# Layer 3 of a four-layer cross-attention and feed-forward network: the experts' work placed in steps between the attention slots of the next chunk, gelu from tanh, four engines in the source's order

## The chip, the cores and the metric

The kernel runs on one core of a Trainium2 chip. The metric is the device time of one execution in microseconds (us); lower is better. A core has TensorE (matrix products into PSUM), VectorE, ScalarE (activations), GpSimd[...] and DMA queues, here all issued by SyncE. Each engine works through its own queue of instructions and waits for the others through semaphores. In the profile the engines are called PE, PEld (TensorE's weight loads), DVE (VectorE), ACT (ScalarE), POOL (GpSimd) and SP (SyncE).

## What is computed

A stream `x` of 2048 tokens by 256 features passes four layers. Each adds a cross-attention over 1601 context rows and then a feed-forward part, both on the layer-normalized `x`:

```python
x = x + L0_xattn(layernorm(x), ctx);  x = x + L0_ffn(layernorm(x))
x = x + L1_xattn(layernorm(x), ctx, mask);  x = x + L1_ffn(layernorm(x))
x = x + L2_xattn(layernorm(x), ctx);  x = x + L2_ffn(layernorm(x))
x = x + L3_xattn(layernorm(x), ctx, ctx, mask);  x = x + L3_ffn(layernorm(x))

# L3_xattn: 16 heads of 16
weights = softmax(where(mask == 0, -inf, Q @ K.T / 4))
return (weights @ V) @ Wo.T + bo

# L3_ffn: 8 experts, each with its own 256 consecutive tokens
h = gelu(tokens @ w1 + b1)          # 256 -> 1024, jax.nn.gelu, the tanh form
y = h @ w2 + b2                     # 1024 -> 256
```

The change touches layer 3 alone (the last two lines of the network). The mask lets each query see only context rows from number 1201 on, so the kernel has a path that works with the 400 rows of that tail.

## The kernel before

All matrix products are in float32, except the one for the softmax maxima, which is in bfloat16. The tokens are worked on in four chunks of 512 (`CH`), a chunk has four tiles of 128 (`TPC`), and `self.x` holds the 16 tiles in SBUF.

**Attention of layer 3, `attention3_tail` (L1415).** The 16 heads form four groups `g` of four heads, each head in its own 32 partitions. A *unit* `u` is a pair (chunk, group): 16 units. The 400 keys are cut into four pieces `kt` of 100. The main loop (L1635) has 64 *slots*, n = 4u + kt. In a slot stand, in this order of the source:

- `scores(u, kt)` (L1560): four matmuls of 512 columns, one for each head, into two PSUM tiles `psc` (two banks each), and two exponentials on ScalarE (L1571) to the tiles `p3`.
- `maxima(n+6, 0)` and `maxima(n+6, 1)` (L1538): for a unit that is one and a half units ahead, two bfloat16 matmuls (L1546) into a `psc` tile, and VectorE's reduction to the maxima (L1550). `values` of the slot before stands between the two.
- `values` (L1574): four matmuls of the exponentials with the values into the bank `pa`. After a unit's last one, ScalarE copies `pa` to `o3` (L1587), and `normalize` is put on the list `tasks`.
- one of: `project(u+2)` in slots with kt = 0 (L1524: a query projection into the bank `pm`, and two ScalarE copies with bias); `shift(u+1)` with kt = 2 (L1554: transposes of the maxima into `pm`, one VectorE addition); or, in the other slots, a task: `normalize` (L1590: a matmul into `pm`, and a ScalarE copy to `ri3`), or one or two steps of the list `later`, which holds `out_project`.
- a piece of `reciprocal` (L1600: 128 columns of `ri3` on VectorE; after the fourth piece a product on GpSimd, L1606, and after a chunk's last unit four `out_project` on the list `later`).
- `out_project(c, i)` (L1610): four matmuls into `pm`, an addition of the bias on GpSimd (L1618), one of PSUM and `x` on VectorE (L1619).
- once per chunk `normed` (L1621): `norm` (L125) for the next chunk: statistics on VectorE (L132, L133), the inverse root on GpSimd (L135, L136), scaling on VectorE (L142), eight transposes into `pm` and two copies on ScalarE (L161, L165).

[...]L1517 gives three `psc` tiles of two banks, one `pm`, one `pa`. L1518 keeps TensorE in the source's order; the order of the other engines' instructions is chosen by a scheduler.

**Experts, `ffn3` (L1669).** It comes after the attention. For each expert `e` the weights come by DMA (three sets of buffers); for every second expert `norm` runs. Eight *up* products (L1702, two matmuls of 256 columns each) are followed by a gelu activation with bias on ScalarE (L1706, function Gelu_apprx_tanh) to `h3`; then for each of two token tiles eight *down* matmuls (L1713) gather in `pa`; GpSimd adds `x` and the bias `b2` to `y` (L1718), VectorE adds `pa` (L1719), and a DMA writes `y` out (L1720). There are two `y` buffers.

Of the kernel before, what the change touches and what calls it, by code (L numbers as in the profile page):

```python
# [14 lines left out]

P = 128
D = 256
NTOK = 2048
NCTX = 1601
NT = NTOK // P  # L20
CH = 512
# [8 lines left out]
TK = 4  # L30
# [9 lines left out]
def drain(gen):  # L40
    if gen is not None:
        for _ in gen:
            pass


def step(gen, n):
    if gen is None:
        return
    for _ in range(n):
        if next(gen, True):  # L50
            return


class Net:
# [70 lines left out]
    def norm(self, c, row_scale=None, rms=False, split=None):  # L125


        nc = self.nc
        st = self.small.tile([P, TPC, 6], F32, name="st")
        mv = self.small.tile([P, TPC, 2], F32, name="mv")  # L130
        for i in range(TPC):
            nc.vector.bn_stats(st[:, i, :], self.x[c * TPC + i])  # L132
            nc.vector.bn_aggr(mv[:, i, :], st[:, i, :])  # L133
        rstd = self.small.tile([P, TPC], F32, name="rstd")
        nc.gpsimd.tensor_scalar_add(rstd, mv[:, :, 1], LN_EPS)  # L135
        nc.gpsimd.tensor_tensor(rstd, rstd, self.mhalf, ALU.pow)  # L136
        if row_scale is not None:
            nc.gpsimd.tensor_tensor(rstd, rstd, row_scale, ALU.mult)
        xns = []
        for i in range(TPC):  # L140
            xn = self.xnp.tile([P, D], F32, name="xn", bufs=4)
            nc.vector.tensor_scalar(  # L142
                xn, self.x[c * TPC + i], mv[:, i, 0:1], rstd[:, i : i + 1], ALU.subtract, ALU.mult
            )
            xns.append(xn)
        if rms:
            ss = self.small.tile([P, TPC], F32, name="ss")
            for i in range(TPC):
                sq = self.xnp.tile([P, D], BF16, name="sq", bufs=1)
                nc.scalar.activation(sq, xns[i], AF.Square, accum_out=ss[:, i : i + 1])  # L150
            ri = self.rms_inverse(ss, D)
            for i in range(TPC):
                nc.vector.tensor_scalar(xns[i], xns[i], ri[:, i : i + 1], None, ALU.mult)
        if split is None:
            xnT = self.xnp.tile([P, 2, CH], F32, name="xnT")
        else:
            xnT = [split.tile([P, 2, CH], F32R, name=f"xn{n}") for n in ("hi", "lo")]
        for kc in range(2):
            ps = self.pm()
            for i in range(TPC):  # L160
                nc.tensor.transpose(  # L161
                    ps[:, i * P : (i + 1) * P], xns[i][:, kc * P : (kc + 1) * P], self.ident
                )
            if split is None:
                nc.scalar.copy(xnT[:, kc, :], ps)  # L165
            else:
                nc.scalar.copy(xnT[0][:, kc, :], ps)
                nc.vector.tensor_tensor(xnT[1][:, kc, :], ps, xnT[0][:, kc, :].bitcast(F32), ALU.subtract)
        return xnT

    def rms_inverse(self, ss, n):

# [1239 lines left out]
                        nc.vector.tensor_tensor(x, ps[:, :D], x, ALU.add)  # L1412


    def attention3_tail(self, mask):  # L1415
        tc, nc, a = self.tc, self.nc, self.a
        H, DH, G = 16, 16, 4
        raw = {}
# [3 lines left out]
        with ExitStack() as s:  # L1422
            kv = s.enter_context(tc.tile_pool(name="kv3", bufs=1))
            qp = s.enter_context(tc.tile_pool(name="q3", bufs=3))
            pp = s.enter_context(tc.tile_pool(name="p3", bufs=6))
            op = s.enter_context(tc.tile_pool(name="o3", bufs=2))


# [42 lines left out]
            with ExitStack() as s0:  # L1471
# [4 lines left out]
                nc.gpsimd.memset(v.rearrange("p k (h e) -> p (k h) e", e=32)[:, :, DH : DH + 1], 1.0)  # L1476
                self.transpose_weight(wkT, raw["Wk"], pad=True)
                self.transpose_weight(wqT, raw["Wq"], pad=True)
                wvT = kv.tile([P, 2, D], F32, name="wvT")
                self.transpose_weight(wvT, raw["Wv"])  # L1480
                nc.vector.tensor_copy(
                    wop.rearrange("p o (h e) -> p (o h) e", e=32)[:, :, 0:DH],
# [31 lines left out]
                        bv[:TR].rearrange("p (h e) -> p h e", e=DH), ALU.add,  # L1514
                    )

            self.banks(s, s=3, m=1, a=1)  # L1517
            s.enter_context(tc.manual_schedule(engines={mybir.EngineType.PE}))  # L1518
            units = [(c, g) for c in range(NCH) for g in range(G)]
            U = len(units)  # L1520
            heads = [slice(32 * j, 32 * j + 32) for j in range(4)]
# [88 lines left out]
            def out_project(c, i):  # L1610
                x = self.x[c * TPC + i]
                ps = self.pm()
                for k in range(G):
                    nc.tensor.matmul(  # L1614
                        ps[:, :D], lhsT=attn[c][:, k, i * P : (i + 1) * P], rhs=woT[:, k, :],
                        start=k == 0, stop=k == G - 1,
                    )
                nc.gpsimd.tensor_tensor(x, x, bo, ALU.add)  # L1618
                nc.vector.tensor_tensor(x, ps[:, :D], x, ALU.add)  # L1619

            def normed(c):  # L1621
                xnT[c] = self.norm(c)


            tasks, later, pieces = [], [], []
            normed(0)
            for u in range(2):
                project(u)
            for n in range(6):
# [4 lines left out]
            last = None  # L1634
            for n in range(U * TK):  # L1635
                u, kt = divmod(n, TK)
                scores(u, kt)
                maxima(n + 6, 0)
                if last is not None:
                    values(*last)  # L1640
                last = (u, kt)
                maxima(n + 6, 1)
                if kt == 0 and u + 2 < U:
                    project(u + 2)
                elif kt == 2 and u + 1 < U:
                    shift(u + 1)
                elif tasks:
                    f, args = tasks.pop(0)
                    f(*args)
                elif later:  # L1650
                    f, args = later.pop(0)
                    f(*args)
                    if kt == 3 and later:
                        f, args = later.pop(0)
                        f(*args)
                if pieces:
                    reciprocal(*pieces.pop(0))
                if n % (G * TK) == TK and u // G + 1 < NCH:
                    normed(u // G + 1)
            values(*last)  # L1660
            for f, args in tasks:
                f(*args)
            for args in pieces:
                reciprocal(*args)
            for f, args in later:
                f(*args)


    def ffn3(self):  # L1669
# [53 lines left out]
@with_exitstack  # L1723
def network(ctx: ExitStack, tc: tile.TileContext, a, out):
    net = Net(ctx, tc, a, out)
    net.load_context()
    masks = ("mask_BxSxS2_ik0", "mask_1x1xSxS2_ik0")
    with tc.tile_pool(name="look", bufs=2) as pool:
        net.attention0(net.look_at_masks(pool, masks))
    net.experts0()  # L1730
    n_odd = net.verdict()
    with tc.If(n_odd == 0) as masked:
        net.attention1_tail("L1_xattn", masks[0])
        net.ffn1()
        net.attention1("L2_xattn", bias=True)
        net.ffn2()
        net.attention3_tail(masks[1])
        net.ffn3()
    with masked.Else():
        net.attention1("L1_xattn", mask=masks[0])  # L1740
        net.ffn1()
        net.attention1("L2_xattn", bias=True)
        net.ffn2()
        net.attention3()
        net.ffn3()
# [35 lines left out]
```

## Time and profile before

| what | us |
|---|---|
| median of 3 runs | 2220.4 (2210.71 to 2221.96) |
| the profiled execution | 2223.65 |
| its span, first to last instruction | 2221.9 |
| first exponential of layer 3's attention | at 1781.7 |
| last exponential of it ends | at 2087.8 |
| stretch with experts alone | 2107.0 to 2221.9 |

The profile's page gives the engines' share of the whole span:

```profile
PE 1968.0 (89%) x8841; PEld 967.7 (44%) x8841; DVE 1209.1 (54%) x2252; ACT 717.5 (32%) x968; POOL 632.3 (28%) x405
...
PEclk9799999999998699999997899999978889799999
```

The first line has busy us, share and number of instructions for each engine. The second cuts the span into 40 equal slices and shows in tenths which share of TensorE's full clock was granted; layer 3 fills about the last eight of them. The shares are means over stages with different limits, so that layer 3 has to be read from its own stretches.

### The profile page before, as it was taken

Reading aid. Unit: us, or ns where it says so; the run is one execution under the profiler, and the core shown is the slowest. Engines: PE = TensorE matmul, PEld = TensorE weight load, DVE = VectorE, ACT = ScalarE, POOL = GpSimd, SP = SyncE. Lnnn points to the kernel's source line nnn. Section 1 sums busy time; section 2 is a strip of 40 time slices with the busy share of each in tenths; the row PEclk is TensorE's granted clock in tenths of the full one; section 3 lists DMA queues with packets and bytes.
Section 4 is the critical chain, followed back from the end, with each engine's and each line's share of the span. In section 5 each row is a group of like instructions: output and inputs, shape, how many; then the busy total and the mean of one; then the engine's idle time right before and its main releaser. Section 6 shows DMA issues by size and latency. Waiting matters only on the chain.

```text
span 2221.9 us, 22832 instructions
## 1 busy us (share of the span) xinstructions
PE 1968.0 (89%) x8841; PEld 967.7 (44%) x8841; DVE 1209.1 (54%) x2252; ACT 717.5 (32%) x968; POOL 632.3 (28%) x405
## 2 busy tenths in 40 slices
PE   7789999999998677789897889999968788989899
PEld 3233333333334422234443674555557422333487
DVE  4565646555552599975645563222076557566500
ACT  4544434344443100000112442111143255455422
POOL 1168878777785000000000021000024401000100
PEclk9799999999998699999997899999978889799999
DMA  8820000000000000000201000000000000000351
GB/s 278 265 83 1 1 1 1 1 1 1 1 1 0 1 0 1 1 0 0 67 0 40 0 1 21 0 1 1 0 0 1 6 1 1 1 1 1 114 188 61
DMA packets 39698, 63.51 MB, mean 29 GB/s; under 512 B 5133, under 2 KB 32158, under 8 KB 39582
## 3 DMA queue, kind: packets, MB, share of 16 engines
q1 hardware_dynamic: 37776, 60.33, 8.4%
q10 hardware_dynamic: 1806, 1.64, 0.2%
q8 instruction: 71, 1.16, 0.2%
q14 instruction: 45, 0.37, 0.1%
HBM read 59.87 MB, written 2.10 MB: 28 GB/s over the span
## 4 chain that ended last, share of the span: by engine, by line
PE 66%; DVE 22%; ACT 4%; issue 3%; DMA 3%; POOL 2%; SPq 0%; DVEq 0%; ACTq 0%; POOLq 0%
PE pa L454 7%; PE psc L442 5%; PE psc L627 5%; PE psc L766 4%; PE pa L786 4%; DVE ge L576 4%; DVE mp L367 4%; PE psc L1564 3%; PE psc L1702 3%; DVE ge L578 2%; PE pa L1713 2%; DVE ri L404 2%; PE pa L1581 2%; DVE ri L1604 2%; PE pm L1614 2%
## 5 line engine op out<-in xcount | busy, mean ns | idle before, releaser
L463 POOL TENSOR_TENSOR sp<-sp,p 128x1024 f32<-128x1024 f32 (+1 forms) x176 | 418.9, 2380 | 59.6 <-ACT p L447 49.0
L367 DVE TENSOR_REDUCE mp<-pm 128x1 f32<-128x512 f32 x384 | 242.6, 679 | 161.4 <-PE pm L362 160.7
L447 ACT ACTIVATE p<-psc 128x1024 f32<-128x1024 f32 (+1 forms) x208 | 212.9, 1024 | 261.1 <-PE psc L442 167.0
L442 PE MATMUL psc<-qT,kT 64*128 64x512 f32 (+1 forms) x832 | 219.9, 591 | 0.0
L454 PE MATMUL pa<-p,v 128*64 128x512 f32 (+1 forms) x832 | 204.2, 613 | 0.0
L593 PE MATMUL psc<-ge,pick 128*8 128x512 bf16 x512 | 142.3, 378 | 37.9 <-DVE ge L576 18.6
L1571 ACT ACTIVATE p<-psc 100x1024 f32<-100x1024 f32 x128 | 125.5, 1023 | 110.1 <-PE psc L1564 104.5
L1550 DVE TENSOR_REDUCE ms<-psc 128x2 bf16<-128x800 f32 x128 | 124.1, 987 | 67.2 <-PE psc L1546 63.0
L362 PE MATMUL pm<-kb,qb 64*128 64x512 bf16 x384 | 100.2, 389 | 26.4 <-DVE mp L367 24.9
L1564 PE MATMUL psc<-q,kT 32*100 32x512 f32 x512 | 97.8, 689 | 14.8 <-DVE ms L1550 10.3
L627 PE MATMUL psc<-w_e,xe 128*128 128x512 f32 x256 | 110.4, 593 | 0.0
L454 PEld LDWEIGHTS pa<-p,v 128*64 128x64 f32 (+1 forms) x832 | 51.1, 137 | 131.6 <-issue 128.6
L135 POOL TENSOR_SCALAR rstd<-mv 128x4 f32<-128x4 f32 x32 | 10.5, 329 | 333.6 <-DVE mv L133 333.6
L829 POOL MEMSET v<- 128x4 f32 x1 | 0.1, 106 | 366.4 <-DVE n_odd L280 366.4
L766 PE MATMUL psc<-q,kT 128*128 128x512 f32 (+1 forms) x208 | 102.2, 610 | 0.0
L576 DVE TENSOR_SCALAR ge<-bc,g 128x128 bf16<-128x128 f32 (+15 forms) x128 | 99.8, 780 | 1.8 <-ACT bc L570 1.8
L142 DVE TENSOR_SCALAR xn<-x,mv,rstd 128x256 f32<-128x256 f32 x128 | 54.3, 482 | 75.0 <-PE pm L161 72.1
L442 PEld LDWEIGHTS psc<-qT,kT 64*128 64x128 f32 (+1 forms) x832 | 85.5, 185 | 19.5 <-issue 6.3
L786 PE MATMUL pa<-v,p 128*128 128x257 f32 (+1 forms) x416 | 93.9, 381 | 0.0
L593 PEld LDWEIGHTS <-pick 128*8 128x8 bf16 x512 | 39.4, 85 | 117.3 <-issue 91.3
L578 DVE TENSOR_SCALAR ge<-bc,g 128x1920 bf16<-128x1920 f32 (+14 forms) x120 | 89.4, 746 | 0.6 <-ACT bc L570 0.6
L440 PE MATMUL psc<-sh,negz 64*128 64x512 bf16 (+1 forms) x416 | 87.1, 383 | 2.6 <-ACT sh L389 2.5
(343 smaller groups left out, 3250.5 us busy)
## 6 DMA issues: line engine op xcount, KB each, us to landing
w<-in_L_ffn_w_dram SPq DMA_DIRECT2D x16, 1024.0 KB, 6.2
head<-in_mask_BxSxS_ik_dram SPq DMA_DIRECT2D x16, 600.5 KB, 4.7
head<-in_mask_1x1xSxS_ik_dram SPq DMA_DIRECT2D x16, 600.5 KB, 4.8
tail<-in_mask_BxSxS_ik_dram SPq DMA_DIRECT2D x16, 200.0 KB, 4.5
tail<-in_mask_1x1xSxS_ik_dram SPq DMA_DIRECT2D x16, 200.0 KB, 3.7
x<-in_x_dram SPq DMA_DIRECT2D x16, 128.0 KB, 3.7
w_e<-in_L_ffn_experts_dram SPq DMA_DIRECT2D x2, 1024.0 KB, 7.2
out_dram<-y SPq DMA_DIRECT2D x16, 128.0 KB, 2.7
```

The source lines that it names most:

```text
L367: nc.vector.tensor_reduce(mp[:, i, j, n : n + 1], pair[j][:, :wd], AX.X, ALU.max)
L442: nc.tensor.matmul(sc[:r, j, :], lhsT=kT[h, hp, kt * P : kt * P + r], rhs=q[h, :], start=False, stop=True,)
L447: nc.scalar.activation(p[:r], sc[:r], AF.Exp, scale=DH**-0.5)
L454: nc.tensor.matmul(acc[h, :], lhsT=v[:r, kt, hp * P + h.start : hp * P + h.stop], rhs=p[:r, j, :], start=kt == 0, stop=kt == NKT - 1,)
L463: nc.gpsimd.tensor_tensor(sums[:r], sums[:r], p[:r], ALU.add)
L576: nc.vector.tensor_scalar(ge[:, :hi], bc[:, :hi], own, None, ALU.is_lt)
L578: nc.vector.tensor_scalar(ge[:, hi:], bc[:, hi:], own, None, ALU.is_le)
L593: nc.tensor.matmul(rk[j // 2][0:E, j % 2, :], lhsT=pick[:, e, :], rhs=ge[:, j * CH : (j + 1) * CH], start=first, stop=last,)
L627: nc.tensor.matmul(sc[:, j, :], lhsT=xnT[t // TPC][:, kc, (t % TPC) * P : (t % TPC + 1) * P], rhs=ew[kc][:, half * 4 + 2 * j : half * 4 + ...
L766: nc.tensor.matmul(sc[:r, j, :], lhsT=kT[:, kc, ks], rhs=q[:, kc, :], start=kc == 0, stop=False)
L786: nc.tensor.matmul(acc[:, : D + 1], lhsT=p[:r, kt, i * P : (i + 1) * P], rhs=v[:r, kt, :], start=kt == 0, stop=kt == NKT - 1,)
L1564: nc.tensor.matmul(sc[j // 2][:TR, j % 2, :], lhsT=kT[h, g, kt * TR : (kt + 1) * TR], rhs=q[u][h, :], start=True, stop=True,)
```

## The change

- `norm` becomes a generator, `norm_steps`, of six steps; `norm` itself runs it through and gives the same instructions.
- `attention3_tail` and `ffn3` (in this path) become one function, `layer3_tail`. All four compute engines are kept in the source's order from the first norm of layer 3's attention on (`IN_ORDER`).
- When the last `out_project` of a chunk has been placed, the list `fbits` gets the chunk's expert work in 38 bits: `begin` and five `norm_step`, then for each of the chunk's two experts eight `up` (two matmuls and a ScalarE copy with bias) and eight `down` (two matmuls), a `down` being four places behind its `up`. Each slot of the loop takes two bits: `feed(1)` between the two maxima, and `feed(1)` at its end. What is left is placed after the loop.
- gelu is taken apart. ScalarE copies the up product with the bias to `h`; after each second `up` GpSimd works out z = h (1 + 0.044715 h²) in three instructions on 128x512; `gelu()`, in the slot after the second maximum, puts tanh(0.798 z) on ScalarE and (z + 1) h on VectorE. The factor 0.5 is in the last addition.
- PSUM: two `psc` tiles (for three), `pm`, `pa`, and one bank each for the up products (`psu`) and the down sums (`psy`).
- SBUF: five `p3` tiles (for six), two sets of expert weights (for three), one `y` (for two). The first two experts' weights are asked for before the loop, those of expert e + 2 when expert e ends.
- In a slot: a piece of `reciprocal` first, then `scores`, `values`, first maximum, fed bit, second maximum, `gelu()`, project, shift or task, one step of `later`, fed bit, one step of the next chunk's norm.

The diff, cut to its core:

```diff
+IN_ORDER = {mybir.EngineType.PE, mybir.EngineType.Activation, mybir.EngineType.DVE, mybir.EngineType.Pool}
...
-            self.banks(s, s=3, m=1, a=1)
-            s.enter_context(tc.manual_schedule(engines={mybir.EngineType.PE}))
+            self.banks(s, s=2, m=1, a=1)
+            psf = s.enter_context(tc.tile_pool(name="ps_f", bufs=1, space=bass.MemoryType.PSUM))
+            wp = s.enter_context(tc.tile_pool(name="f3w", bufs=2))
+            hp = s.enter_context(tc.tile_pool(name="f3h", bufs=2))
...
+            for e in range(2):
+                load_expert(e)
+            s.enter_context(tc.manual_schedule(engines=IN_ORDER))
...
+                if i == TPC - 1:
+                    fbits.extend(feed_forward(c))
...
+                def up(e, f, k):
...
+                    for kc in range(2):
+                        nc.tensor.matmul(
+                            ps, lhsT=w1[:, kc, (f + k) * P : (f + k + 1) * P],
+                            rhs=out[0][:, kc, (e % 2) * 256 : (e % 2 + 1) * 256],
+                            start=kc == 0, stop=kc == 1,
+                        )
+                    at = e * NF + f + k
+                    h = state["h"][:, f : f + 2, :]
+                    nc.scalar.activation(h[:, k, :], ps, AF.Identity, bias=b1[:, at : at + 1])
+                    if k == 1:
+                        z = hp.tile([P, 2, 256], F32, name="z3")
+                        nc.gpsimd.tensor_tensor(z, h, h, ALU.mult)
+                        nc.gpsimd.tensor_scalar(z, z, 0.044715, 1.0, ALU.mult, ALU.add)
+                        nc.gpsimd.tensor_tensor(z, z, h, ALU.mult)
+                        gelus.append((h, z))
...
+                def end(e):
+                    b2 = experts.pop(e)[2]
+                    for i in range(2):
+                        t = 2 * e + i
+                        y = hp.tile([P, D], F32, name="y", bufs=1)
+                        nc.gpsimd.tensor_tensor(y, self.x[t], b2, ALU.add)
+                        nc.vector.scalar_tensor_tensor(y, state["acc"][:, i, :], 0.5, y, ALU.mult, ALU.add)
+                        nc.sync.dma_start(self.out[0, t * P : (t + 1) * P, :], y)
+                    if e + 2 < E:
+                        load_expert(e + 2)
...
+                yield begin, ()
+                for _ in range(5):
+                    yield norm_step, ()
+                for e in (2 * c, 2 * c + 1):
+                    for f in range(0, NF + 4, 2):
+                        for k in range(2):
+                            if f < NF:
+                                yield up, (e, f, k)
+                        for k in range(2):
+                            if f >= 4:
+                                yield down, (e, f - 4, k)
...
+            def gelu():
+
+                if gelus:
+                    h, z = gelus.pop(0)
+                    nc.scalar.activation(z, z, AF.Tanh, scale=0.7978845608028654)
+                    nc.vector.scalar_tensor_tensor(h, z, 1.0, h, ALU.add, ALU.mult)
...
             for n in range(U * TK):
                 u, kt = divmod(n, TK)
+                if pieces:
+                    reciprocal(*pieces.pop(0))
                 scores(u, kt)
-                maxima(n + 6, 0)
                 if last is not None:
                     values(*last)
                 last = (u, kt)
+                maxima(n + 6, 0)
+                feed(1)
                 maxima(n + 6, 1)
+                gelu()
...
-                elif later:
+                if later:
                     f, args = later.pop(0)
                     f(*args)
...
+                feed(1)
+                if n % (G * TK) == 0 and u // G + 1 < NCH:
+                    norming = self.norm_steps(u // G + 1, xn)
+                step(norming, 1)
             values(*last)
+            feed(1)
+            gelu()
+            feed(1)
             for f, args in tasks:
                 f(*args)
-            for args in pieces:
-                reciprocal(*args)
-            for f, args in later:
+            while pieces:
+                reciprocal(*pieces.pop(0))
+                feed(2)
+                gelu()
+            while later:
+                f, args = later.pop(0)
                 f(*args)
+                feed(1)
+            while fbits:
+                ready = len(gelus)
+                feed(2)
+                for _ in range(ready):
+                    gelu()
...
-        net.attention3_tail(masks[1])
-        net.ffn3()
+        net.layer3_tail(masks[1])
```

## The prediction

> **What bounds the kernel now.** I read four views. First the table of stretches for the last stage: the span from the first exponential of layer 3 (1781.7) to the last one (2087.8), and what follows. Columns: busy us and (x instructions) of TensorE, its weight loads, VectorE, ScalarE, GpSimd; granted clock; DMA share; GB/s.
>
> ```profile
> 1781.70:1904.90 123.20, 110.46 (x598) 33.59 (x597) 76.72 (x92) 67.72 (x82) 12.28 (x13) 0.88 0.00 1
> 1904.90:2055.00 150.10, 137.45 (x731) 46.02 (x730) 95.90 (x122) 76.53 (x91) 12.66 (x12) 0.87 0.00 1
> 2055.00:2087.80 32.80, 29.46 (x182) 11.13 (x180) 16.24 (x26) 17.63 (x20) 3.80 (x4) 1.00 0.01 1
> 2087.80:2107.00 19.20, 14.78 (x73) 10.50 (x71) 11.14 (x25) 5.17 (x9) 2.88 (x5) 1.00 0.77 253
> 2107.00:2221.90 114.90, 110.60 (x512) 94.19 (x512) 8.17 (x20) 31.77 (x68) 11.22 (x15) 1.00 0.41 133
> ```
>
> The 64 attention slots take 306.1 us (4.8 each) with TensorE some 90% busy at a clock of 0.87, the last 134.1 us are a 19 us changeover and then experts that are TensorE alone at full clock (512 matmuls, 110.6 us, 13.8 per expert). GpSimd is nearly idle. So there is little empty TensorE time to put the experts into: about 30 us of gaps and what the clock loses.
>
> Second, the groups of instructions in the loop and in the expert stage, for durations (columns: busy, mean ns, idle before and its releaser):
>
> ```profile
> L1571 ACT ACTIVATE p<-psc 100x1024 f32<-100x1024 f32 x128 | 125.5, 1023 | 110.1 <-PE psc L1564 104.5 <-PE psc L1546 5.5
> L1550 DVE TENSOR_REDUCE ms<-psc 128x2 bf16<-128x800 f32 x116 | 113.2, 987 | 62.8 <-PE psc L1546 58.6 <-PE psc L1564 3.5
> L1606 POOL TENSOR_TENSOR attn<-o,ri 128x512 f32<-128x512 f32 x15 | 19.0, 1266 | 211.5 <-DVE ri L1604 205.1 <-ACT p L1571 6.4
> ...
> L1706 ACT ACTIVATE h<-psc,b 128x256 f32<-128x256 f32 x64 | 30.2, 474 | 66.0 <-PE psc L1702 66.0
> L1718 POOL TENSOR_TENSOR y<-x,b 128x256 f32<-128x256 f32 x16 | 11.6, 728 | 98.1 <-DMA out_dram<-y 64.4 <-issue 24.6 <-PE pm L161 9.0
> ```
>
> Third, the timeline of one slot: scores 1.12 us, a pair of exponentials starting 1.24 us after the scores, two reductions.
>
> ```profile
> 1862.64 1.12 PE L1564 MATMUL psc<-q,kT 32*100 32x512 f32 x8
> ...
> 1863.88 1.94 ACT L1571 ACTIVATE p<-psc 100x1024 f32<-100x1024 f32 x2 [0.54 <-PE psc L1564]
> ...
> 1866.74 1.83 DVE L1550 TENSOR_REDUCE ms<-psc 128x2 bf16<-128x800 f32 x2
> ```
>
> Fourth, stretches of 3.4 us: where four reciprocals in a row (3.4 us on VectorE) hold up the reductions, TensorE goes part idle and its clock is halved next.
>
> ```profile
> 1847.60:1851.00 3.40, 2.62 (x14) 0.57 (x16) 3.15 (x5) 1.02 (x1) 1.26 (x1) 0.82 0.00 0
> 1851.00:1854.40 3.40, 3.40 (x18) 0.87 (x19) 2.00 (x2) 1.02 (x1) 0.00 (x0) 0.50 0.00 0
> ```
>
> **What the Trainium skill says.** PSUM — Partial Sum Buffer, "Engine vs sequencer instructions": the queues of ScalarE, VectorE and GpSimd are strict FIFO; so an activation that waits holds all behind it. No row shows it directly, the new order makes it decisive. TensorE: Matmul & The Clock Gate, Part 1: an idle window halves the clock; the two lines above agree in kind (2.62 of 3.40 busy, then 0.50). ScalarE: Activation LUTs, "Table sets": exp and tanh share a set, gelu has its own; the trace has one 1.28 us table load before the first exponential and one before the first gelu (2105.24); the second goes.
>
> **The change part by part.** Times below are at full clock. Names: S scores 1.05, V values 1.0, M0 and M1 maxima 0.34 each, F1 and F2 the two fed bits of a slot (4 expert matmuls each, 6.91/8 = 0.86), X the slot's extra (project 1.98, shift 0.40, normalize 1.07), L an out-projection 2.0.
>
> *Slots with nothing fed (n = 0 to 24).* PSUM buffers for scores and maxima fall from three to two, so the second half of S waits for the reduction of M1: S 1.05, V 1.0, M0 0.39 to the start of its reduction, two reductions 1.83, hand-overs 0.1: 4.4 us. X, one reciprocal (0.91) and the norm steps fit beside. 25 x 4.4 = 110. The single bank for X, L and norm transposes makes L wait for X's copies: slots 21 to 24 cost 11 more, the transposes of the norm in 4, 5, 20 and 21 some 9 more. Sum 130, against 120.8 now (exponential of slot 0 at 1781.71, of slot 25 at 1902.54).
>
> *Where feeding falls.* A chunk's bits are begin, five norm steps, and per expert 8 up and 8 down: 38. The first is taken at the end of slot 24, so every bit with k=1 comes in the middle of a slot, and gelu() follows it in the same slot. Slots 25 to 63 hold 79 bits: chunks 0 and 1 (four experts) whole, and half of the experts' work is left for after the loop.
>
> *An up slot.* The tanh is put on ScalarE right behind the bias copy whose polynomial GpSimd has still to work out. From exponential to exponential: exponential 1.02, M0 0.40, up 0.86, to ScalarE 0.1, bias copy 0.47 (the gelu row's shape), GpSimd: two products of 1.27 (attn row), one tensor_scalar, hand-overs 0.25; tanh 0.61, next bias copy and hand-overs 0.6. The tensor_scalar on 128x512 is in no row: between 0.52 and 1.27 us; I take 0.62, that of a one-input GpSimd cast of this shape (L672). The tanh likewise: between the 0.586 of a copy and 0.685 with a bias column; I take 0.61. Sum 7.3 us. Behind the waiting tanh stand X's copies, the next bias copy and both next exponentials; M0 and the next up wait for those. TensorE needs some 5.5 of the 7.3. X's copies add 1.4 in a project slot, 0.6 in a normalize slot. 16 up slots in the loop: 16 x 7.3 + 6 x 1.4 + 4 x 0.6 - 8 x 0.4 (no bias copy follows) = 124. In slots 36, 37, 38, 40 and 56 L or a norm transpose needs the bank whose copy stands behind the tanh: 1.6 to 5.6 each, 19 together. 143.
>
> *A down slot* has no tanh: S, exponential, M0, F1, M1, F2 give 4.9, plus X (project 1.8, normalize 0.85, shift 0.2). 16 slots: 78, X 5, L in 39, 53, 54: 8. The last one of an expert ends it with y in one buffer: the second addition waits for the first y's DMA (2.7 to land) on GpSimd, the VectorE instruction behind it waits too, and M1's reduction with it: 4.5 more in three slots (in the fourth no reduction is left), 13.5; without reductions 3 less. 102.
>
> *Norm slots* (25 to 27, 44 to 46): VectorE steps of 1.0 to 1.2 between the two reductions: 35. Slot 63: 3.5.
>
> Loop: 130 + 143 + 102 + 35 + 3.5 = 414 against 306: +108.
>
> *After the loop.* Four experts remain. The same immediate gelu() stands between the last reciprocals, and the out-projections' bank is freed by VectorE behind the waiting products: expert 4 ends 38 us after the last exponential. In the last while loop products are taken an iteration later, so GpSimd bounds: y wait 4.3, four polynomials of 3.3, tanh to product 1.5, last down 1.8: 20.8 per expert (13.8 now). Expert 5 ends at 59; chunk 3's norm, behind the second y, ends at 72; expert 6 at 91, expert 7 at 112; two y in turn 7.5: 120 against 134: -14. The weights' DMAs (SP, 2.1 MB an expert, 6.2 to land) hide under the expert before; without that cover some 4 each.
>
> *Clock.* An up slot leaves TensorE idle up to 2.8 us at a stretch. Between nothing (all at full clock) and +86 (32 pairs of up at half clock, M0 and up 1.2 more on the chain: 38; and 16 down slots 3 more: 48). I take half of the pairs: +19.
>
> Sum: +108 - 14 + 19 = +113 on the profiled execution's span 2221.9 (its own time 2223.65; the runs' median is 2220.4): 2335.
>
> **The rivals.**
> - *The one-bank and y waits are hidden, the clock holds:* what the traces show for it is that now such waits (DMA out_dram, 64.4 us) cost nothing; against it, they stand in strict order now. Takes away 19 + 13.5 + 12 (y after the loop) of +94: 2271.
> - *TensorE goes cold through both parts:* for it, 0.50 already after a window 77% busy; against, the down slots are dense. +94 + 86: 2402.
> - *Faster: TensorE stays the bound at full clock, the polynomial done before the tanh is reached.* TensorE's work in the loop: 67 + 64 + 39 (S, V, M) + 51 (X) + 24 (L) + 7 (norms) + 55 (half of the experts) = 307, about today's 306, since the split reciprocals end the halved clock; afterwards GpSimd's 4 x 14.7 and 23 for start and end: 82 for 134. 2172. For it: GpSimd is idle and 13% of the clock is lost today. Against: the order of the bits. It decides once an up pair costs 2.9 us less than above (94/32), a slot of 4.4.
>
> **How the numbers follow.** Forecast 0.52, milder 0.20, colder 0.15, faster 0.13 (of which and of the milder case 0.03 within 0.5%). A measurement of this kernel tells a change from none at about 0.5%. Slower 0.85. The range 2260 to 2410 takes in the milder and colder cases and the bounds of the clock; the faster one is left out.
>
> **What would show it.** Right: in the loop ScalarE waits for GpSimd before each tanh some 3.4 us; up slots near 7.3 us, down slots near 5; VectorE waits for GpSimd's y, and that for the DMA, about 4 us per expert; expert 4 begins only after the loop; one table load fewer. Wrong: tanh without wait, slots under 5.3, GpSimd's polynomial well under 3 us, or a loop near 306 us with the clock at 1.0.

## The result, and the profile after

The kernel after the change takes 2361.35 us (median of 4 runs, 2350.77 to 2372.57), the kernel before, beside it, 2221.18. The ratio is 1.064 (95% interval 1.057 to 1.070): slower by 6%, where 2335 was predicted and 2260 to 2410 given as the range. The profiled execution is the slowest of the four, 2372.57 us; its span is 2370.7.

First the table of stretches of the kernel after, cut where the prediction's sums cut it: slots 0 to 24, slots 25 to 63 (in which experts are fed), and what follows the last exponential. The columns are those of the prediction's first table. In the kernel before, the same stretches took 120.8, 185.3 and 134.1 us, at a clock of 0.87, 0.90 and 1.00.

```profile
1775.80:1923.80 148.00, 123.49 (x607) 38.14 (x610) 77.08 (x108) 66.02 (x81) 10.34 (x12) 0.85 0.00 1
1923.80:2220.90 297.10, 241.33 (x1180) 108.00 (x1172) 129.78 (x177) 120.94 (x165) 73.87 (x79) 0.89 0.10 30
2220.90:2370.70 149.80, 94.85 (x312) 64.71 (x310) 32.01 (x60) 28.12 (x55) 62.51 (x67) 0.79 0.14 45
```

The loop has grown from 306.1 to 445.1 us. The slots in which nothing is fed yet went from 120.8 to 148, with nothing more to compute than before. And what follows the loop, although half of the experts' work is gone from it, did not shrink: 149.8 for 134.1, with TensorE at 0.79 of its clock where the experts had 1.00 before.

The groups of instructions in the loop, those that wait (busy us, mean ns of one | idle us ahead of them and what ended it):

```profile
L1580 PE MATMUL psc<-kb,qb 32*128 32x400 bf16 x232 | 40.2, 366 | 32.7 <-ACT p L1605 28.2 <-DVE ms L1584 3.9
...
L1692 POOL TENSOR_TENSOR z<-z,h 128x512 f32<-128x512 f32 x16 | 20.3, 1269 | 1.3
...
L1690 POOL TENSOR_TENSOR z<-h 128x512 f32<-128x512 f32 x16 | 16.8, 1048 | 118.1 <-ACT h L1687 118.1
...
L1735 ACT ACTIVATE z<-z 128x512 f32<-128x512 f32 x16 | 10.1, 630 | 51.5 <-POOL z L1692 51.5
L1691 POOL TENSOR_SCALAR z<-z 128x512 f32<-128x512 f32 x16 | 9.9, 621 | 1.4
...
L1713 POOL TENSOR_TENSOR y<-x,b 128x256 f32<-128x256 f32 x7 | 5.1, 727 | 49.8 <-DMA out_dram<-y 49.8
```

Three waits stand out. Each of the 16 tanh (L1735) keeps ScalarE idle 51.5 / 16 = 3.2 us until GpSimd's last product (L1692). The matmuls of the maxima (L1580) wait 32.7 us, mostly for an exponential. GpSimd's additions for `y` (L1713) wait for the DMA of an earlier `y`. In the kernel before, the row of the maxima waits 3.3 us:

```profile
L1546 PE MATMUL psc<-kb,qb 32*128 32x400 bf16 x230 | 42.7, 362 | 3.3 <-ACT p L1571 1.6
```

The timeline of one slot with an up step in it, slot 30:

```profile
1957.59 1.94 ACT L1605 ACTIVATE p<-psc 100x1024 f32<-100x1024 f32 x2
...
1960.11 0.47 ACT L1687 ACTIVATE h<-psu,b 128x256 f32<-128x256 f32 x1 [0.58 <-PE psu L1680]
...
1960.66 1.04 POOL L1690 TENSOR_TENSOR z<-h 128x512 f32<-128x512 f32 x1 [4.47 <-ACT h L1687]
...
1961.52 1.12 PE L1598 MATMUL psc<-q,kT 32*100 32x512 f32 x8
1961.78 0.62 POOL L1691 TENSOR_SCALAR z<-z 128x512 f32<-128x512 f32 x1
1962.49 1.28 POOL L1692 TENSOR_TENSOR z<-z,h 128x512 f32<-128x512 f32 x1
...
1963.80 0.63 ACT L1735 ACTIVATE z<-z 128x512 f32<-128x512 f32 x1 [3.22 <-POOL z L1692]
1964.34 1.92 ACT L1605 ACTIVATE p<-psc 100x1024 f32<-100x1024 f32 x2
...
1965.39 0.36 PE L1580 MATMUL psc<-kb,qb 32*128 32x400 bf16 x2 [1.76 <-ACT p L1605]
```

The scores of the next slot end at 1962.64. Their exponentials could start then, but they stand behind the tanh and start at 1964.34, 1.7 us later; the maxima, which need the exponentials' tile back, let TensorE stand idle for 1.76. From exponential to exponential the slot lasts 6.75.

Last, the timeline after the loop: the end of expert 5, up steps of expert 6, and one of expert 7:

```profile
2299.90 0.38 SPq L1546 DMA_DIRECT2D w<-in_L_ffn_w_dram  x1
2299.96 0.42 DVE L1714 SCALAR_TENSOR_TENSOR y<-psy,y 128x256 f32<-128x256 f32 x1 [2.14 <-PE psy L1701]
2300.41 0.49 SPq L1715 DMA_DIRECT2D out_dram<-y  x1
2306.05 0.72 POOL L1713 TENSOR_TENSOR y<-x,b 128x256 f32<-128x256 f32 x1 [8.93 <-DMA out_dram<-y]
...
2311.30 1.44 PE L173 MATMUL pm<-ident,xn 128*128 128x128 f32 x4 [11.43 <-DVE xn L151]
...
2319.11 0.47 ACT L1687 ACTIVATE h<-psu,b 128x256 f32<-128x256 f32 x1 [2.17 <-PE psu L1680]
...
2319.63 2.08 PE L1680 MATMUL psu<-xnT,w 128*128 128x256 f32 x4 [0.56 <-ACT h L1687]
...
2321.75 0.47 ACT L1687 ACTIVATE h<-psu,b 128x256 f32<-128x256 f32 x1 [2.17 <-PE psu L1680]
...
2343.11 1.13 PE L1680 MATMUL psu<-xnT,w 128*128 128x256 f32 x4 [0.57 <-ACT h L1687]
```

The second `y` (2306.05) waits 5.6 us from the issue of the first one's DMA (2300.41), which has the 1 MB load of a later expert's weights just ahead of it in SyncE's queue (2299.90). Then the up steps: there is one bank `psu`, so that each waits 0.56 us after the last one's matmuls for ScalarE to copy them out. In expert 6, which begins after a norm for which TensorE stood idle for 11.43 us, six ups in a row run at half clock (2.08 us for four matmuls; the clock from 2314.4 to 2329.6 is 0.50), and one takes 2.64 us with its wait. In expert 7 the same wait stands between ups at full clock (1.13 us), and one takes 1.7. So the wait alone does not halve the clock. The prediction's price for four expert matmuls was 0.86.

### The profile page after: what moved, and what is told of

Its sections match the earlier page's. It is cut to its first block, busy times and chain, and to the rows that moved or that the text cites. A ratio compares the mean times of both kernels' runs of the same rounds, so it can differ in the third digit from the quotient of the medians.

```text
span 2370.7 us, 22935 instructions
## 1 busy us (share of the span) xinstructions
PE 2021.5 (85%) x8831; PEld 983.0 (41%) x8841; DVE 1234.7 (52%) x2284; ACT 733.0 (31%) x999; POOL 724.9 (31%) x501
## 4 chain that ended last, share of the span: by engine, by line
PE 63%; DVE 20%; ACT 6%; DMA 4%; POOL 4%; issue 3%; SPq 0%; ACTq 0%; DVEq 0%; POOLq 0%
PE pa L468 6%; PE psc L456 5%; PE psc L641 5%; PE psc L780 4%; PE pa L800 4%; DVE ge L590 4%; PE psc L1598 3%; PE psu L1680 3%; DVE mp L381 3%; DVE ge L592 2%; DVE ri L418 2%; PE psy L1701 2%; ACT p L1605 2%; PE pm L1565 2%; PE pm L1648 2%
## 5 line engine op out<-in xcount | busy, mean ns | idle before, releaser
L477 POOL TENSOR_TENSOR sp<-sp,p 128x1024 f32<-128x1024 f32 (+1 forms) x176 | 418.7, 2379 | 60.1 <-ACT p L461 49.4
L1680 PE MATMUL psu<-xnT,w 128*128 128x256 f32 x256 | 88.0, 475 | 14.8 <-ACT h L1687 14.8
L1598 PE MATMUL psc<-q,kT 32*100 32x512 f32 x512 | 93.6, 677 | 8.1 <-DVE ms L1584 5.7
L1736 DVE SCALAR_TENSOR_TENSOR h<-z,h 128x512 f32<-128x512 f32 x32 | 25.5, 798 | 122.2 <-ACT z L1735 122.2
```

The costliest lines, as they stand in the source:

```text
L477: nc.gpsimd.tensor_tensor(sums[:r], sums[:r], p[:r], ALU.add)
L1598: nc.tensor.matmul(sc[j // 2][:TR, j % 2, :], lhsT=kT[h, g, kt * TR : (kt + 1) * TR], rhs=q[u][h, :], start=True, stop=True,)
L1680: nc.tensor.matmul(ps, lhsT=w1[:, kc, (f + k) * P : (f + k + 1) * P], rhs=out[0][:, kc, (e % 2) * 256 : (e % 2 + 1) * 256], start=kc == 0, ...
```

## The experiments

My theory after the result: four separate waits, each put in by one decision of the change. (1) The third tile for scores and maxima was given up, so the scores wait for a reduction and the maxima for an exponential. (2) The tanh is queued at once. (3) The `y` DMA. (4) One bank for the up products. The rivals to each: keeping the order on four engines costs it; the experts' own work on TensorE costs it; the polynomial on GpSimd bounds the stage.

Lengths below are read from each profile, "loop" from the first exponential's start to the last one's end, "after" from there to the end of the span. The ratio is to the runs of the kernel before beside each group (medians 2217.6, 2221.0 and 2221.0). With two tiles, slots 0 to 24 came out near 144 or near 148 us in different profiled executions, so a few us in the loop are only read where these agree or from slots 25 to 63.

| kernel | time, us | ratio to before (interval) | loop | slots 0-24 | slots 25-63 | after |
|---|---|---|---|---|---|---|
| before | 2221 | 1 | 306.1 | 120.8 | 185.3 | 134.1 |
| changed | 2361 | 1.064 (1.057 to 1.070) | 445.1 | 148.0 | 297.1 | 149.8 |
| e1 tanh a slot later | 2328 | 1.050 (1.048 to 1.052) | 401.6 | 147.9 | 253.7 | 145.3 |
| e2 SyncE in order | 2352 | 1.060 (1.057 to 1.063) | 432.2 | 144.5 | 287.7 | 136.5 |
| e3 nothing fed | 2419 | 1.089 (1.085 to 1.092) | 352.2 | 143.7 | 208.5 | 289.1 |
| e4 no polynomial | 2306 | 1.041 (1.036 to 1.046) | 399.9 | 144.0 | 256.0 | 127.7 |
| e5 before, two tiles | 2310 | 1.041 (1.037 to 1.045) | 387.7 | 163.7 | 224.0 | 141.7 |
| e6 before, in order | 2198 | 0.990 (0.987 to 0.994) | 280.1 | 116.1 | 164.0 | 137.4 |
| e7 new slots, three tiles | 2200 | 0.991 (0.989 to 0.994) | 282.6 | 115.3 | 167.3 | 139.1 |
| e8 four banks after the loop | 2364 | 1.064 (1.061 to 1.068) | 445.5 | 148.0 | 297.5 | 139.9 |
| e9 e7, out-projections as before | 2186 | 0.985 (0.982 to 0.987) | 266.5 | 106.7 | 159.8 | 137.7 |
| e10 fed, all mended | 2296 | 1.033 (1.029 to 1.036) | 384.9 | 147.0 | 237.9 | 125.7 |
| e11 changed again | 2366 | 1.067 (1.064 to 1.069) | 436.3 | 144.5 | 291.8 | 149.8 |

**e1, the tanh one slot later.**

```diff
                 maxima(n + 6, 0)
+                ready = len(gelus)
                 feed(1)
                 maxima(n + 6, 1)
-                gelu()
+                for _ in range(ready):
+                    gelu()
```

> The tanh and its product are put into a slot only for a pair whose polynomial was asked for in an earlier slot; all else as in the changed kernel. Theory (the tanh stands in ScalarE's queue right behind a polynomial that GpSimd has still to work out): ScalarE's wait for GpSimd before the tanh in the loop goes from some 3 us each to nearly none, up slots fall from 6.7-8.2 to about 5.3, and the five slots in which an out-projection or a norm transpose stood behind it (13.0 to 15.3) to about 9: some 60 us less, about 2300 in all, still slower than before. Rival (TensorE's own work at its lower clock fills those slots anyway): under 15 us less, 2345 or more.

The loop fell by 43.5 us, all of it in slots 25 to 63; the median by 33, where about 60 had been expected. The timeline of e1, at slot 30:

```profile
1960.22 0.47 ACT L1687 ACTIVATE h<-psu,b 128x256 f32<-128x256 f32 x1 [0.58 <-PE psu L1680]
...
1960.59 0.62 ACT L1735 ACTIVATE z<-z 128x512 f32<-128x512 f32 x1
...
1962.85 1.94 ACT L1605 ACTIVATE p<-psc 100x1024 f32<-100x1024 f32 x2 [1.64 <-PE psc L1598]
```

The tanh no longer waits, and the exponential now waits for its scores. The clock in slots 25 to 63 rose from 0.89 to 0.95. The tanh's place costs 43.5 us, and the loop is still 95 longer than before: (2) is one cause of several.

**e2, SyncE's queue in the source's order too.**

```diff
-IN_ORDER = {mybir.EngineType.PE, mybir.EngineType.Activation, mybir.EngineType.DVE, mybir.EngineType.Pool}
+IN_ORDER = {mybir.EngineType.PE, mybir.EngineType.Activation, mybir.EngineType.DVE, mybir.EngineType.Pool, mybir.EngineType.SP}
```

> The DMAs of SyncE are kept in the source's order too, so that an expert's y goes out before the weights of expert e+2 are asked for. Theory (y with one buffer waits for a DMA that lies behind a megabyte of weights): from issue to landing the first y takes about 2 us instead of 5.5, GpSimd's second addition comes 3.5 us sooner for each of six experts, some 20 us less, about 2340. Rival (the y wait is hidden, or the weights now come too late for expert e+2): no change within 5 us, or slower.

Now both `y` go out ahead of the next loads (timeline of e2 at the end of expert 5):

```profile
2286.51 3.41 SPq L1715 DMA_DIRECT2D out_dram<-y  x2
2288.37 0.72 POOL L1713 TENSOR_TENSOR y<-x,b 128x256 f32<-128x256 f32 x1 [5.16 <-DMA out_dram<-y]
...
2290.02 0.39 SPq L1545 DMA_DIRECT2D w<-in_L_ffn_w_dram  x1
```

From the issue of the first `y` to the addition that waits for it are 1.9 us, not 5.6. The stage after the loop lost 13.3 us, the loop itself 4.1 (against e11, whose slots 0 to 24 ran alike). The spans differ by 14.8 us from e11 and 21.8 from the changed kernel's first profile, the medians by 14 and 9: the mechanism is shown; its worth lies between 9 and 22 us, near 15 where slots 0 to 24 ran alike, less than the 20 expected.

**e3, nothing fed in the loop.** The two `feed(1)` of a slot are left out; all experts are worked on after the loop.

> No expert work is fed into the attention slots; all eight experts come after the loop, in the form they have there. Theory (two costs apart: the new slots of the attention themselves, with two PSUM tiles and four engines in order, and the experts in GpSimd's chain): the loop takes about 345 us (306 before, 445 in the changed kernel), so that the attention alone is slower than before, and the experts after it about 24 us each instead of 14, some 215 in all: about 2340. Rival (the feeding alone is what costs in the loop): loop about 306.

The loop came out close to what was expected (352.2 for 345), the stage after it far longer (289.1 for 215), and with it the time (2419 for 2340). It gives the first split of the loop: 46 us over the kernel before with no expert work in it. And eight experts with tanh and one `psu` bank take 289 us after the loop, where with the gelu table the stage took 134.

**e4, no polynomial.** This kernel leaves out gelu's polynomial on GpSimd and the product on VectorE: `h` is one tanh straight from the up product.

> gelu is left out and replaced by one tanh with bias out of PSUM: no polynomial on GpSimd, no product on VectorE, no wait of ScalarE for GpSimd; matmuls and slots as in the changed kernel. Theory: up slots about 5, experts after the loop 15 to 17 us instead of 22 to 25: about 100 us less, near 2260. Rival (what is lost is TensorE's clock and the PSUM banks): 30 us less or fewer.

The loop is nearly the same as with the tanh a slot later (399.9 and 401.6; 256.0 and 253.7 in slots 25 to 63): the polynomial costs the loop nothing that could be seen except through the wait of the tanh. After the loop it is worth 22 us. Together 55 in the median, far less than the 100 expected.

**e5, the kernel before with two tiles; e6, the kernel before with its order kept on four engines.** One line each:

```diff
-            self.banks(s, s=3, m=1, a=1)
+            self.banks(s, s=2, m=1, a=1)
```

```diff
-            s.enter_context(tc.manual_schedule(engines={mybir.EngineType.PE}))
+            s.enter_context(tc.manual_schedule(engines={mybir.EngineType.PE, mybir.EngineType.Activation, mybir.EngineType.DVE, mybir.EngineType.Pool}))
```

> The kernel before with two PSUM tiles for scores and maxima in place of three, nothing else. With nothing fed, the changed kernel's loop still takes 352 us against 306 before, and its plain slots 3.80 and 4.53 where before has 3.20 and 3.62. If the missing third tile makes that (the second half of the scores waits for the second reduction of the slot before), the loop here takes 340 to 350 and the time 2255 to 2265. If the order on ScalarE, VectorE and GpSimd makes it, the loop stays within 6 us of 306 and the time within 0.4% of before.

> The kernel before with the source's order kept on TensorE, ScalarE, VectorE and GpSimd in layer 3's attention, three tiles, nothing else moved. If the third tile is what counts, the loop stays near 306, or below it by up to 25, since the order puts one reciprocal in a slot where the planner had put four in a row (slots of 11.6 to 13.4 us): 2195 to 2230. If keeping the order costs the 46 us of the changed kernel's unfed loop, the time is 2255 or more.

These two part the theory from its rival. Two tiles alone make the kernel before 4.1% slower, more than expected (388 for 340 to 350): its slots 0 to 24 run at a clock of 0.73, where the kernel before has 0.87. The order alone makes it 1.0% faster. So the order is no cost but a gain, and the 46 us of e3 are a third tile's loss with the order's gain taken off.

**e7, the new slots with three tiles, nothing fed, experts as before.** `psf`, the feeding and the experts are taken out of `layer3_tail`, which has `self.banks(s, s=3, m=1, a=1)` again, and `ffn3` follows it. The five `p3` tiles stay.

> The changed kernel's attention slots, in their new order on four engines, with three tiles and nothing fed, and the experts after it as they were before (gelu from its table, 134 us after the loop). Third-tile theory: the loop comes down from 352 to about 310, the time is within 15 us of 2222. If the new order of the slot costs it, the loop stays near 350 and the time is about 2265.

The loop is 282.6, even below the expected 310 (and the time 21 us below before, outside the 15 given), and e3's is 352.2: in the new order the third tile is worth 69.6 us. Scores and maxima in the loop, first e7, then e3:

```profile
L1578 PE MATMUL psc<-q,kT 32*100 32x512 f32 x504 | 85.9, 649 | 9.0 <-ACT p L1585 8.4 <-DVE ms L1564 0.4
...
L1560 PE MATMUL psc<-kb,qb 32*128 32x400 bf16 x230 | 28.3, 337 | 1.6 <-ACT p L1585 1.6
```

```profile
L1598 PE MATMUL psc<-q,kT 32*100 32x512 f32 x504 | 101.2, 680 | 10.1 <-DVE ms L1584 9.8 <-ACT p L1605 0.2
L1580 PE MATMUL psc<-kb,qb 32*128 32x400 bf16 x232 | 38.2, 365 | 27.0 <-ACT p L1605 26.0
```

The maxima's wait for an exponential grows from 1.6 to 27.0 us. The scores wait about as long with two tiles as with three, but for a reduction. The timelines of a plain slot of each show it. First e7, then e3 (scores L1578 and L1598):

```profile
1852.61 0.61 PE L1560 MATMUL psc<-kb,qb 32*128 32x400 bf16 x4
...
1853.79 1.39 PE L1578 MATMUL psc<-q,kT 32*100 32x512 f32 x8 [0.24 <-ACT p L1585]
```

```profile
1857.71 0.25 PEld L1598 LDWEIGHTS psc<-q,kT 32*100 32x100 f32 x4 [1.02 <-DVE ms L1584]
1857.71 2.00 PE L1598 MATMUL psc<-q,kT 32*100 32x512 f32 x8 [0.77 <-DVE ms L1584]
...
1858.61 0.25 PEld L1598 LDWEIGHTS psc<-q,kT 32*100 32x100 f32 x4 [0.65 <-DVE ms L1584]
```

With two tiles both halves of the scores wait for a reduction of the maxima (0.77 and then some 0.6 us), and the eight matmuls stretch over 2.00 us for 1.39. Of the 69.6 us, TensorE's idle time in the loop gives 23 (30.3 to 53.3); its busy time gives 47 (252.3 to 298.9) for the same matmuls, at a clock of 0.88 and 0.89 in the two parts for 0.96 and 0.97.

**e8, after the loop each pair of ups in the two banks of a score tile.**

```diff
-                        state["ps"] = psf.tile([P, 2, 256], F32, name="psu", tag="u")
-                    ps = state["ps"][:, k, :]
+                        state["ps"] = self.psc() if tail else psf.tile([P, 2, 256], F32, name="psu", tag="u")
+                    ps = state["ps"][:, k, :256]
```

> The changed kernel; only after the loop each up step's two results lie in the two banks of a score tile (two tiles in turn), in place of one bank in which each up waits for the bias copy before it (0.56 us, at half clock 2.64 an up). If that wait and the halved clock it brings make the 150 us after the loop, these fall by 20 to 30, to about 2335. If GpSimd's polynomial (3.1 a pair) and the chain from it to the down steps bound the stage, they fall by less than 10.

The stage is 9.9 us shorter: at the upper edge of the second case. Expert 6 has three ups at or near half clock, not six. The median, 2364, is no better than the changed kernel's. **e11** is the changed kernel, run once more:

> The changed kernel once more, beside the others on one chip: its four runs lay between 2351 and 2373, too far apart to say whether e8's banks (2364, its stage after the loop 10 us shorter in the profile) brought anything. If they did, it lies near 2372; if not, near 2362.

It took 2366 (2363.9 to 2370.6), between the two. Its stage after the loop is 149.8 us again, so the 9.9 in the stage hold; its loop was 9 us shorter than e8's, with the same instructions in it, which hides them in the total. On totals alone e8 stays unclear.

**e9, e7 with the old rule for out-projections.**

```diff
-                if later:
+                elif later:
                     f, args = later.pop(0)
                     f(*args)
+                    if kt == 3 and later:
+                        f, args = later.pop(0)
+                        f(*args)
```

> As e7 (new slot order, order kept on four engines, three tiles, nothing fed, experts as before), but an out-projection only goes into a slot without project or shift, two in the fourth slot, as the kernel before has it. In e7 the six slots that take an out-projection beside a project or shift (slots 22, 24, 38, 40, 54, 56) last 7.4 to 9.7 us; in e6, which has the old rule, the ones with two out-projections last 7.07 and the norms in one piece cost 12 to 14 in slots 4, 20 and 36. If each of these is what it looks like, the loop falls from 282.6 to 255 to 268 and the time to 2172 to 2190, below e6 and e7. If the out-projections cost the same wherever they stand, it stays within 6 us of 2200.

Loop 266.5, time 2186: within both expected ranges. So an out-projection in a slot with a projection or shift stretches it; that the one bank `pm`, which both need, is the reason was not tried by itself. Its stretches (loop, in the same two parts):

```profile
1780.40:1887.10 106.70, 96.72 (x588) 29.82 (x591) 75.23 (x102) 65.14 (x80) 9.41 (x11) 0.97 0.00 1
1887.10:2046.90 159.80, 148.83 (x924) 49.61 (x916) 116.72 (x165) 95.41 (x114) 25.31 (x29) 1.00 0.00 1
```

TensorE is busy 245.6 of 266.5 us, at a clock of 0.97 and 1.00. This is the fastest version here, 1.5% below the kernel before and about 7% below the changed one.

**e10, feeding with all four waits mended** (two `y` buffers; `b1` moved so that they fit, and transposed before the loop).

> The changed kernel with all that the runs before named taken out at once: each tanh a slot later, SyncE's queue in order too, two buffers for y, and after the loop the up steps in the two banks of a score tile. Two score tiles remain. If the costs add (44 and 13 in the loop, 10 and up to 15 after it), it takes 2275 to 2300, still slower than before, because the missing third tile alone is 70 us. If one of them covered for another, 2310 to 2330. If feeding was sound apart from them, 2220 or less.

2296, in the range for costs that add. Its stretches:

```profile
1783.00:1930.00 147.00, 123.14 (x606) 38.09 (x609) 76.50 (x106) 65.75 (x79) 10.33 (x12) 0.85 0.00 1
1930.00:2167.90 237.90, 219.06 (x1180) 98.06 (x1173) 132.67 (x185) 121.34 (x165) 76.68 (x80) 0.97 0.11 34
2167.90:2293.60 125.70, 87.88 (x312) 61.80 (x310) 29.15 (x53) 27.87 (x55) 62.65 (x66) 0.82 0.19 62
```

In slots 25 to 63 TensorE is now busy 219 of 238 us at 0.97: there is little left to fill. Still the loop is 118 longer than e9's, and the stage after it only 12 shorter.

## Why the prediction came out as it did

Where the 139 us of the loop come from, each step between two measured kernels: the order, with the slots rearranged, 306.1 to 282.6, -23.5 (e7); the third tile, +69.6 (e3); half of the experts fed with the tanh in a later slot, +49.4 (e1); the tanh at once, +43.5 (changed). Of the 49.4, 4.3 stand in slots 0 to 24, where both kernels do the same; 45.1 in slots 25 to 63 are the cost of feeding, and some 16 of these go in e10, with the `y` wait mended. The sizes hold for this sequence of steps: in the kernel before, with its own order, the third tile was worth 81.6 (e5). The stage after the loop: 134.1 to 149.8; the two mends of e2 (-13.3) and e8 (-9.9) add up to 23.2, and e10, which has both, is 24.1 shorter.

Point by point, in the prediction's own terms:

- *The tanh behind the bias copy, up slots of 7.3 us.* Right, though the terms as listed add up to 7.5. ScalarE waits 3.2 us for each tanh (3.4 predicted); plain up slots last 6.7 to 7.2 (slots 30, 47, 49, 50), those with X's copies 7.8 to 9.2 (28, 29, 48). Down slots without anything else came to 5.0 to 5.8 for 4.9 (33 to 35). The rival without this wait was priced at 2.9 us an up pair, 47 for the 16 in the loop; e1 measured 43.5. The polynomial's three durations were 1.05, 0.62 and 1.27; the 0.62 taken for the unseen tensor_scalar, and 0.61 for the tanh (0.63), held, and the product of `h` with itself was the one overpriced.
- *Slots 25 to 63 as a whole.* 414 - 130 = 284 predicted, before the clock; 297.1 and, in e11, 291.8 measured. Norm slots (25 to 27, 44 to 46), put at 35, took 41.4, as one `y` wait of some 6 falls into slot 44; the up and down slots with slot 63, put at 248.5, took 255.9. The longest is slot 54 with 17.6 us: an out-projection and a `y` wait together.
- *The `y` wait, 4.5 us in three slots.* The mechanism right, and 13.5 close to the 16 that e10 saves in slots 25 to 63 (slots 36, 44 and 54 fell by 5.1, 6.1 and 7.0 against e1). But it rested on a landing of 2.7 us. It took 5.6, because the weights' loads, which were costed at nothing as hidden, stand ahead of it in the queue. The trace of the kernel before had this already: 2.7 is the median of its 16 `y`, and four that were issued some 0.5 us after a 1 MB load (at 2119.92, 2133.77, 2147.61 and 2161.46) took 5.3 to 5.6. The Trainium skill, DMA: Bandwidth & Descriptors, "Queues, rings and completion order", says that each DMA engine consumes a queue's descriptors in ring order; e2 agrees: 1.9 us with the `y` first. Loads that nobody waits for are not free for what is queued behind them.
- *Slots with nothing fed, 130 us.* This term failed: 148 (144.5 in e11). The chain was the right one, and plain slots came out at 3.8 to 4.5 for the 4.4 predicted. Wrong was "X, one reciprocal and the norm steps fit beside": the projection slots 4, 8 and 12 took 10.0, 8.0 and 7.0 us (7.2, 4.9 and 4.8 in e7). The clock was then costed only where experts are fed, though it is lower here too: 0.85 (0.88 in e11), and 0.96 in e7, which does the same work with three tiles. The Trainium skill, TensorE: Matmul & The Clock Gate, "A second HAM failure mode: psum-queue depth-cycling", describes a like case for bfloat16 products of 512 columns: short pauses between groups of matmuls, as PSUM banks are cycled, let the clock drop again and again. The runs agree in kind, e5 most plainly: 0.73 in slots 0 to 24 with two tiles in the kernel before, for 0.87 with three. That the pauses are what lowers the clock here was not tried by itself.
- *After the loop, 120 us.* This is the step that failed most, 149.8. Counted at each expert's first `y`, expert 4 ended 54 us after the last exponential, not 38; expert 5 came 25 us later, not 21; expert 6, with a norm ahead of it, 42 later, not 32; expert 7, 22 later, not 21. The sum took GpSimd as the bound at 20.8 an expert. Its `y` wait was too short, and it had no term for the up steps among themselves: the single bank `psu` with a copy between any two, and the halved clock. With the `y` wait mended and the banks apart, e10 takes 125.7, and its experts 5 to 7 follow one another by 22, 32 and 22 us, close to the 21, 32 and 21 predicted. Expert 4 still ends at 45, not 38; where these 7 us come from stays open.
- *The clock, +19.* Not measured by itself. The loop's clock outside slots 0 to 24 rises from 0.89 to 0.95 once the tanh waits are gone, so part of the 43.5 is clock.

So 2335, built on a span of 2221.9, came 26 us below the median and 36 below the span of the profiled execution, 2370.7. The two failed terms were 18 and 30 us too low; the terms for slots 25 to 63 with the whole of the clock (284 + 19 for 297) were 6 too high, and the loop starts 6 earlier (1775.8 for 1781.7): 18 + 30 - 6 - 6 = 36.

Two of the prediction's signs also came true: expert 4 began only after the loop, and the second table load is gone. Its "clock of 0.87" for the loop before is the middle stretch's; the loop as a whole had 0.89.

Of the rivals, the milder one (2271) took the one-bank and `y` waits for hidden, and they weren't. The colder one (2402) had TensorE cold through both parts; its clock was 0.89 where experts are fed and 0.79 after the loop. The faster one failed by more than the tanh: it summed TensorE's work in the loop with half of the experts to 307 us; e10, with the tanh out of the way, has TensorE busy 342 us in the loop. Against e9's 245.6 the busy time grew by 97, not by the 55 that it counted (matmuls at half clock and those spread out by waits are in it). What remains is the main point: most of what the loop before seemed to waste was not idle time that other work could fill. e9's loop is 39.6 us shorter with no expert in it. TensorE's idle time gives only 8 of these (28.7 to 21.0); its busy time gives 32 (277.4 to 245.6) for the same matmuls, with the clock of the two parts at 0.97 and 1.00 for 0.87 and 0.90. The prediction had named both, "about 30 us of gaps and what the clock loses"; e9 wins a good part of both back with no expert moved.

Open: how much of the third tile's 69.6 us the waits would cost at full clock, and how much the clock adds; and whether any way of feeding that keeps three tiles would pay. Neither was tried; three tiles, `pm` and `pa` take eight banks, as many as the change has in all with `psu` and `psy`.

## What to carry to other kernels

Before other work is put into an engine's idle time, find out whether the idle time is an order that can be mended: here one line that keeps the source's order gave 1%, and the change that moved an estimated 55 us of work into the gaps, and gave up a PSUM tile for it, lost 6%. Count a buffer that is given up as a cost in every iteration, those with nothing new in them too. In strict order, place a consumer far enough behind its producer that it need not wait, and a small transfer that something waits for ahead of large ones that nothing waits for. Read the single values behind a median: the slow landing was in the trace of the kernel before.

## What the runs showed of the hardware

- The same instructions in slots 0 to 24 of the changed kernel took 148.0 us (clock 0.85) in one profiled execution and 144.5 (0.88) in another (e11), and the whole loop 445.1 and 436.3. Of the other kernels with these slots, two ran like the first within 0.2 us (e1, e8), and three like e11 within 0.9 (e2, e3, e4). What decides between the two was not found.
- Giving up one of three PSUM tiles lowered the clock of the kernel before from 0.87 to 0.73 in slots 0 to 24 and from 0.90 to 0.86 in slots 25 to 63, with the same instructions to do (e5).
- After TensorE had stood idle for 11.43 us, the first six ups of expert 6 ran at half clock (2.08 us for four matmuls) with a wait of 0.56 us between any two; with that wait between pairs only (e8), three did. The same waits in expert 7, without such a pause ahead, left the clock full (1.13).
- A 128 KB store that was issued 0.5 us after a 1 MB load took 5.6 us until the instruction that waits for it could start, and 1.9 with the store first (e2).
- GpSimd's product of a 128x512 tile with itself took 1.05 us, with another tile 1.27, and a tensor_scalar on it 0.62 (means of 16 in the loop).
